# A graph and mixture-of-experts layer: first expert blocks placed inside the last GNN chunk, with two weight buffers in place of three

## Chip, cores and metric

The kernel runs on one core of a Trainium2 chip. The metric is the device time of one launch in microseconds (us), the median of several runs. Engines are named as the profile names them: PE (TensorE matmul), PEld (its weight load), DVE (VectorE), ACT (ScalarE), POOL (GpSimd) and SP (SyncE, which here issues most DMA transfers).

## What is computed

There are N = 3125 nodes with C = 256 features and 103125 sorted edges. The layer normalizes x, adds up each node's neighbours, runs a gated recurrent cell and a fully connected layer on the sum, adds a small attention-like mix, and then sends every node through two of eight experts. Cut to what matters:

```python
xn = _layernorm(x)
agg = segment_sum(xn[src], dst)
h = relu(agg @ W_rel + b_rel + xn @ W_root)
i, f, g, o = split(h @ W_ih.T + b_ih + b_hh, 4)
c = sigmoid(i) * tanh(g)
x = x + (sigmoid(o) * tanh(c)) @ W_fc + b_fc + mix(xn)
xt = _layernorm(x)
probs = softmax(xt @ Wr + br)              # 8 experts
top_p, top_idx = top_k(probs, 2)
weights = top_p / top_p.sum()
xe = _layernorm(xt) * ln_g[e] + ln_b[e]    # per expert e
y = gelu(xe @ W1[e] + b1[e]) @ W2[e] + b2[e]   # 256 -> 1024 -> 256
out = x + sum over the two chosen experts of weights * y
```

All of it is float32.

## The kernel before

**Stages.** The edge stage builds adjacency tiles and multiplies them with the nodes (L612 to L654), up to about 355 us. Then follows a conditional, `tc.If(total > 0)` at L656, a slow path for unsuitable edge lists that these inputs don't take. Then comes the GNN stage, in chunks of TQ = 4 tiles of P = 126 tokens (`chunk`, L720): six chunks of four tiles, and a seventh of one tile. Then a plan of blocks is made (L890 to L963), and then comes the expert stage (`block`, L970).

**One chunk.** PE computes hT from aggT (L737, with `root` added by DVE at L739), the gates (L747, with sigmoid and tanh on ACT at L749), and the output rows (L765, L768, added by DVE at L770). The rows are normalized (L204) and stored into `acc_dram` (L773), on which the experts later accumulate. The second half of a chunk, the routing, is a generator's remainder: it runs inside the next chunk's gates. It computes the logits (L795 on DVE; in the last two chunks L808 on PE, by way of the transposed lT), softmax and top two, counts with two small matmuls which slot of its expert each token gets (L856, L857; `first` is where an expert's slots begin, `seen` what has been handed out), and scatters each tile's rows into `xs_dram` by two indirect DMAs on POOL (L872, called puts here). Tokens of an expert e lie in rows e*R onward, in the order of arrival.

**One block.** A block is 256 rows of one expert. SP loads the weights w1 (L992), w2 (L993) and the bias b2s (L995), of 1024, 1024 and 128 KB, and the rows xs (L1006). PE transposes xs (L1010), DVE scales the result into xe (L1014), PE multiplies by w1 into PSUM (L1020), ACT applies Gelu into hf (L1022), PE multiplies by w2 (L1033), DVE adds b2s and multiplies by the gate (L1036, L1037), and POOL adds the result into `acc_dram` by an indirect DMA (L1038). Blocks 0 to 7 are the first 256 slots of the experts. The blocks from 8 on are given out by the plan, so their expert and place are read from a register, and after every fourth of them comes a half block of 128 rows. 24 full and four half blocks run in any case; the conditionals at L1050 and L1053 after them are not taken. The last step copies `acc_dram` to the output.

**Buffers.** The pool `ew` holds w1, w2 and b2s three times; `ffn` holds xs three times and its other tiles twice. PSUM has two `ps_tr`, three `ps_mm` and three `ps_o` buffers. The pools `gnn` and `rt` of the GNN stage end before `plan` and `ffn` begin, and their memory is used again.

**What sets the order.** The program is written in the order of the source; a scheduler then places each engine's instructions in one static order, by its own estimate of what is ready. Each engine and each queue works through its order one by one, so an instruction that waits holds up all that stand behind it on the same engine. SP's order around the change is: xT and root of chunk 0, xT of chunk 1, wrows, the conditional, base of two chunks, then the weights of blocks 0, 1 and 2 with root of chunk 1 between.

Of the kernel before, what the change touches and what calls it, by code (L numbers as in the profile page):

```python
# [9 lines left out]
F32 = mybir.dt.float32  # L10
# [8 lines left out]
C = 256  # L19
P = 126  # L20
T = 25
# [24 lines left out]
ROW = C + NE + 1  # L46
XROWS = NE * R + SB
KS = 2 * KC + KF

# [14 lines left out]
def gps_layer(  # L64
# [409 lines left out]
    first = keep.tile([128, 1, NE], F32, name="first")  # L474
    nc.gpsimd.tensor_scalar(first[:, 0, :], cols[:, :NE], float(R), None, op0=OP.mult)
    token = keep.tile([P, T], I32, name="token")
    nc.gpsimd.iota(token, pattern=[[P, T]], base=0, channel_multiplier=1)
# [235 lines left out]

    ew = ctx.enter_context(tc.tile_pool(name="ew", bufs=3, side="right"))
    with tc.tile_pool(name="gnn", bufs=1) as hp, tc.tile_pool(name="rt", bufs=2) as rp:
# [4 lines left out]
        def chunk(t0, pending):  # L720
# [21 lines left out]
            for m in range(KH):  # L742
# [12 lines left out]
                if m == 1 and n > 2 * P:  # L755

                    with tc.issue_after(mm.ins):
                        for _ in pending:
                            pass
            xl = rp.tile([P, TQ, C], F32, name="xl")  # L760
            rows = rp.tile([P, TQ, ROW], F32, name="rows")
            for i, t in enumerate(ts):
# [4 lines left out]
                for k in range(KC):  # L767
# [6 lines left out]
                              base[:, :nt, :])  # L774
            for _ in pending:
                pass
            yield
# [21 lines left out]
            else:  # L799
                lT = rp.tile([128, KC, CT], F32, name="lT", bufs=1)  # L800
                for k in range(KC):
# [46 lines left out]
            if ts[-1] == T - 1:  # L848
                nc.vector.tensor_scalar(chosen[:, nt - 1, :], chosen[:, nt - 1, :], valid, None,
                                        op0=OP.mult)  # L850
            prior = rp.tile([P, TQ, NE], BF16, name="prior")
            for i in range(nt):
# [10 lines left out]
            for r in range(2):  # L863
# [30 lines left out]
    with tc.tile_pool(name="plan", bufs=1) as lp:  # L894
# [68 lines left out]
        nc.vector.tensor_copy(used_i[:, 1:2], hends[:, 0, NE - 1:])  # L963


    SP = (mybir.EngineType.SP,)
    NH = SB // 128
    with tc.tile_pool(name="ffn", bufs=2) as fp:
        def block(b, half=False):

            nh = 1 if half else NH
            ns = 128 * nh
            if b < NE and not half:
                begin, e = b * R, b
                xs_b, w1_b, w2_b = xs_dram[begin:begin + SB, :], W1[e], W2[e]
                b2_b = b2[e:e + 1, :]
                is_e = None
            else:
                if half:
                    of, is_e = (hbegin_i, hwho_i), is_hwho[:, b:b + 1, :]  # L980
                    j = b
                else:
                    j = b - NE
                    of, is_e = (begin_i, who_i), is_who[:, j:j + 1, :]
                begin, e = (nc.values_load(v[0:1, j:j + 1], engines=SP, min_val=0, max_val=most)
                            for v, most in zip(of, (NE * R, NE - 1)))
                xs_b = xs_dram[ds(begin, ns), :]
                w1_b, w2_b = (w[ds(e, 1), :, :].rearrange("o r m -> (o r) m") for w in (W1, W2))
                b2_b = b2[ds(e, 1), :]
            w1 = ew.tile([128, KC, HID], F32, name="w1")  # L990
            w2 = ew.tile([128, KF, C], F32, name="w2")
            nc.sync.dma_start(w1, w1_b.rearrange("(k p) m -> p k m", p=128))  # L992
            nc.sync.dma_start(w2, w2_b.rearrange("(k p) m -> p k m", p=128))  # L993
            b2s = ew.tile([128, C], F32, name="b2s")
            nc.sync.dma_start(b2s, b2_b.to_broadcast([128, C]))  # L995
            if is_e is None:
                sm = small[:, :, b]
            else:
                all_ = fp.tile([128, KS, NE], F32, name="all_")
                nc.vector.tensor_tensor(all_, small,  # L1000
                                        is_e.to_broadcast([128, KS, NE]), OP.mult)
                sm = fp.tile([128, KS], F32, name="sm")
                nc.vector.tensor_reduce(sm, all_, AX.X, OP.add)
            lng, lnb, b1s = sm[:, :KC], sm[:, KC:2 * KC], sm[:, 2 * KC:]
            xs = fp.tile([128, NH, ROW], F32, name="xs", bufs=3)[:, :nh, :]
            nc.sync.dma_start(xs, xs_b.rearrange("(h p) c -> p h c", p=128))  # L1006
            pt = ps_tr()
            for k in range(KC):
                for h in range(nh):
                    nc.tensor.transpose(pt[:, k * ns + h * 128:k * ns + h * 128 + 128],  # L1010
                                        xs[:, h, 128 * k:128 * k + 128], ident)
            xe = fp.tile([128, KC, SB], F32, name="xe")[:, :, :ns]
            for k in range(KC):
                nc.vector.tensor_scalar(xe[:, k, :], pt[:, k * ns:(k + 1) * ns],  # L1014
                                        lng[:, k:k + 1], lnb[:, k:k + 1], op0=OP.mult, op1=OP.add)
            hf = fp.tile([128, KF, SB], F32, name="hf")[:, :, :ns]
            for m in range(KF):
                pm = ps_mm()[:, :ns]
                for k in range(KC):
                    nc.tensor.matmul(pm, w1[:, k, 128 * m:128 * m + 128], xe[:, k, :],  # L1020
                                     start=(k == 0), stop=(k == KC - 1))
                nc.scalar.activation(hf[:, m, :], pm, AF.Gelu, bias=b1s[:, m:m + 1])  # L1022
            for h in range(nh):
                if is_e is None:
                    gate = xs[:, h, C + e:C + e + 1]
                else:
                    gate = fp.tile([128, 1], F32, name="gate", bufs=4)
                    scr = fp.tile([128, NE], F32, name="scr", bufs=4)
                    nc.vector.scalar_tensor_tensor(scr, xs[:, h, C:C + NE], 1.0, is_e[:, 0, :],  # L1029
                                                   op0=OP.mult, op1=OP.mult, accum_out=gate)  # L1030
                po = ps_o()[:, :C]
                for m in range(KF):
                    nc.tensor.matmul(po, hf[:, m, 128 * h:128 * h + 128], w2[:, m, :],  # L1033
                                     start=(m == 0), stop=(m == KF - 1))
                y = fp.tile([128, C], F32, name="y", bufs=4)
                nc.vector.tensor_tensor(y, po, b2s, OP.add)  # L1036
                nc.vector.tensor_scalar(y, y, gate, None, op0=OP.mult)  # L1037
                nc.gpsimd.indirect_dma_start(  # L1038
                    out=acc_dram[:, :],
                    out_offset=bass.IndirectOffsetOnAxis(ap=xs[:, h, C + NE:].bitcast(I32), axis=0),  # L1040
                    in_=y, in_offset=None, compute_op=OP.add)

        for b in range(SURE):
            block(b)
            if b >= NE and (b - NE) % HSURE == HSURE - 1:
                block((b - NE) // HSURE, half=True)
        used = nc.values_load(used_i[0:1, 0:1], min_val=0, max_val=ND)  # L1047
        hused = nc.values_load(used_i[0:1, 1:2], min_val=0, max_val=NE)
        for b0, b1 in ((SURE, SURE + 2), (SURE + 2, NBLK)):
            with tc.If(used > b0 - NE):  # L1050
                for b in range(b0, b1):
                    block(b)
        with tc.If(hused > HSURE):  # L1053
            for b in range(HSURE, NE):
                block(b, half=True)
    nc.sync.dma_start(out, acc_dram[:N, :])
# [59 lines left out]
```

## Time and profile before

| | |
|---|---|
| median of 3 runs | 1149.16 us (1146.96 to 1151.12) |
| profiled execution | 1149.45 us, its span 1147.7 us |
| PE busy | 1057.1 us, 92% of the span |
| DVE, ACT, POOL busy | 553.6, 427.5, 169.7 us |
| L747 (gates), PE | 257.8 us, 672 passes |
| L1020 and L1033 (experts), PE | 189.4 and 184.2 us |
| DMA moved | 161.43 MB, 141 GB/s in the mean |
| weight loads w | 56 of 1024 KB |

A matmul in float32 appears as two passes, so 16 matmuls of a block's up-projection are "x32". In a row of the timeline the columns are start, duration over the merged instructions, engine, line, operation, output and inputs, shape, count, and in brackets the idle time of the engine before it with what ended that. Rows of one engine overlap a little, since a matmul's end is modelled and the next one starts before it. A row of stages has the stretch, its length, then busy time and count for PE, PEld, DVE, ACT and POOL, then the granted clock, the share of DMA time and GB/s. The granted clock is a share of TensorE's full speed. The page's chain of waits reaches back only from the end to 1120 us, so the stages have to be read one by one.

### The profile page before, as it was taken

The page shows a single profiled execution, that of the slowest core. Times are in us where ns is not written, and L with a number is a line of the kernel's source. Part 1 is how long each engine was busy: PE and PEld are TensorE (multiplying, and loading weights), DVE is VectorE, ACT ScalarE, POOL GpSimd, SP SyncE. Part 2 cuts the span into 40 slices and gives each one's busy share as a digit, 9 for nine tenths or more (in the row PEclk, how much of TensorE's full clock was granted, in tenths as well). Part 3 has the DMA queues.
Part 4 walks back from the last instruction along what each step waited for, and adds up shares of the span by engine and source line. Part 5 has one row for each costly group of instructions (what it writes and reads, how often), then busy time and mean ns, then how long its engine had stood idle before and what let it go on. Part 6 is the DMA issues. An engine that isn't in the chain of part 4 may idle for free. (4 is left out here: it accounts for less than half of the span.)

```text
span 1147.7 us, 15551 instructions
## 1 busy us (share of the span) xinstructions
PE 1057.1 (92%) x5613; PEld 807.3 (70%) x5613; DVE 553.6 (48%) x1767; ACT 427.5 (37%) x936; POOL 169.7 (15%) x153
## 2 busy tenths in 40 slices
PE   5799999999999999999999998299999999899992
PEld 2357988988996454545454557288888888788881
DVE  5757788788761184848383937411112222222210
ACT  3454755755732233334333336122222232222220
POOL 2220000000001002020202021212212222122221
PEclk9889999999999999999999999599999999999996
DMA  7884965963007521213121111157666676666734
GB/s 230 293 278 131 252 168 130 253 170 96 1 1 239 176 91 38 91 38 91 38 91 37 36 38 46 52 147 201 188 193 189 187 235 184 201 188 193 227 65 126
DMA packets 121148, 161.43 MB, mean 141 GB/s; under 512 B 9570, under 2 KB 109320, under 8 KB 120870
## 3 DMA queue, kind: packets, MB, share of 16 engines
q1 hardware_dynamic: 108156, 144.40, 41.0%
q0 software_dynamic: 12064, 15.08, 7.1%
q8 instruction: 49, 0.80, 0.3%
q10 hardware_dynamic: 840, 0.83, 0.2%
q14 instruction: 39, 0.32, 0.1%
HBM read 101.37 MB, written 62.10 MB: 142 GB/s over the span
## 5 line engine op out<-in xcount | busy, mean ns | idle before, releaser
L747 PE MATMUL ps_mm<-hT,wih 128*128 128x504 f32 (+1 forms) x672 | 257.8, 543 | 1.6 <-ACT act L749 1.6
L747 PEld LDWEIGHTS ps_mm<-hT,wih 128*128 128x128 f32 x672 | 120.3, 190 | 133.8 <-issue 127.9
L1020 PE MATMUL ps_mm<-xe,w 128*128 128x256 f32 (+1 forms) x896 | 189.4, 369 | 3.3 <-DVE xe L1014 3.3
L1033 PE MATMUL ps_o<-w,hf 128*128 128x256 f32 x832 | 184.2, 379 | 0.0
L1020 PEld LDWEIGHTS ps_mm<-xe,w 128*128 128x128 f32 x896 | 161.6, 192 | 27.0 <-DVE xe L1014 6.6
L630 PE MATMUL ps_o<-A,hi 126*128 126x252 f32 (+1 forms) x650 | 176.3, 305 | 0.8 <-ACT A L392 0.7
L1033 PEld LDWEIGHTS ps_o<-w,hf 128*128 128x128 f32 x832 | 157.8, 190 | 21.3
L630 PE MATMUL ps_o<-A,lo 126*128 126x252 f32 (+1 forms) x650 | 161.2, 281 | 0.0
L1022 ACT ACTIVATE hf<-ps_mm,sm 128x256 f32<-128x256 f32 (+1 forms) x160 | 71.7, 453 | 199.2 <-PE ps_mm L1020 197.5
L392 ACT CAST A<-ps_mm 126x450 fp32r<-126x450 f32 x175 | 93.8, 538 | 99.8 <-PE ps_mm L390 98.2
L1038 POOL DMA_INDIRECT acc_dram<-y,xs x52 | 80.4, 1546 | 318.8 <-DVE scr L1029 131.6
L630 PEld LDWEIGHTS ps_o<-A,hi 126*128 126x128 f32 x650 | 124.9, 192 | 2.8 <-ACT aggT L638 1.7
L384 DVE TENSOR_TENSOR hr<-two,rowT 128x756 bf16<-128x756 bf16 x175 | 95.9, 548 | 62.9 <-PE ps_mm L390 62.4
L630 PEld LDWEIGHTS ps_o<-A,lo 126*128 126x128 f32 x650 | 125.2, 193 | 0.0
L390 PE MATMUL ps_mm<-hk,hr 128*126 128x150 bf16 x1050 | 102.2, 233 | 12.7 <-DVE hk L384 12.4
L384 DVE TENSOR_TENSOR hk<-two,keyT 128x900 bf16<-128x900 bf16 x175 | 108.8, 622 | 0.0
L390 PEld LDWEIGHTS <-hr 128*126 128x126 bf16 x1050 | 91.2, 137 | 18.7 <-DVE hk L384 16.5
L1036 DVE TENSOR_TENSOR y<-ps_o,b2s 128x256 f32<-128x256 f32 x52 | 22.1, 425 | 163.9 <-PE ps_o L1033 163.9
L749 ACT ACTIVATE act<-ps_mm,bg 128x504 f32<-128x504 f32 (+1 forms) x84 | 52.6, 634 | 107.3 <-PE ps_mm L747 107.2
L795 DVE SCALAR_TENSOR_TENSOR scr<-xl,wrows 126x256 f32<-126x256 f32 x160 | 75.5, 472 | 3.3
L872 POOL DMA_INDIRECT xs_dram<-rows,at_i x50 | 52.6, 1052 | 127.9 <-DVE at_i L869 110.9
L1022 ACT ACTIVATE hf<-ps_mm,small 128x256 f32<-128x256 f32 x64 | 29.8, 474 | 76.4 <-PE ps_mm L1020 76.4
(250 smaller groups left out, 920.1 us busy)
## 6 DMA issues: line engine op xcount, KB each, us to landing
w<-in_W_dram SPq DMA_DIRECT2D x56, 1024.0 KB
xs_dram<-blank SPq DMA_DIRECT2D x3, 7022.5 KB
xs_dram<-blank SPq DMA_DIRECT2D x1, 6757.5 KB
xs<-xs_dram SPq DMA_DIRECT2D x24, 265.0 KB
root_dram<-hr SPq DMA_DIRECT2D x24, 252.0 KB
root<-root_dram SPq DMA_DIRECT2D x6, 1008.0 KB
b2s<-in_b_dram SPq DMA_DIRECT2D x28, 128.0 KB
xn_dram<-xn SPq DMA_DIRECT2D x5, 630.0 KB
```

The source lines that it names most:

```text
L384: row = nc.vector.tensor_tensor(to[:, :m], two[:, :, :w, :].to_broadcast([128, m, w, GH]), of[:, g:g + m, None, :].to_broadcast([128, m, w ...
L390: mm = nc.tensor.matmul(pa[:P, i * DT:(i + 1) * DT], hr[:, i, :, h], hk[:, i, :, h], start=(h == 0), stop=(h == GH - 1))
L392: copy = nc.scalar.copy(A[:, :, c0:c0 + m * D], pa[:P, :m * DT].rearrange("p (d t) -> p t d", t=T))
L630: last = nc.tensor.matmul(pg[k][:, :n], of[:, t, 128 * k:128 * k + 128], A[:, t, :n], start=(t == 0 and of is hi), stop=(t == T - 1 and of ...
L747: mm = nc.tensor.matmul(pm[:, :n], wih[:, k, i, 128 * m:128 * m + 128], hT[:, k, :n], start=(k == 0), stop=(k == KH - 1))
L749: nc.scalar.activation(act[:, i, :n], pm[:, :n], AF.Tanh if gate == 2 else AF.Sigmoid, bias=bg[:, gate, m:m + 1])
L795: nc.vector.scalar_tensor_tensor(scr, xl[:, i, :], 1.0, wrows[:, e, :], op0=OP.mult, op1=OP.mult, accum_out=lg[:, i, e:e + 1])
L872: put = nc.gpsimd.indirect_dma_start(out=xs_dram[:, :], out_offset=bass.IndirectOffsetOnAxis(ap=at_i[:w, i:i + 1], axis=0), in_=rows[:w, i ...
L1020: nc.tensor.matmul(pm, w1[:, k, 128 * m:128 * m + 128], xe[:, k, :], start=(k == 0), stop=(k == KC - 1))
L1022: nc.scalar.activation(hf[:, m, :], pm, AF.Gelu, bias=b1s[:, m:m + 1])
L1033: nc.tensor.matmul(po, hf[:, m, 128 * h:128 * h + 128], w2[:, m, :], start=(m == 0), stop=(m == KF - 1))
L1038: nc.gpsimd.indirect_dma_start(out=acc_dram[:, :], out_offset=bass.IndirectOffsetOnAxis(ap=xs[:, h, C + NE:].bitcast(I32), axis=0), in_=y, ...
```

## The change

The change has four parts. In the chunk after which 2520 tokens have been routed (the fifth), a new function `ahead` counts how many of the first 256 slots of experts 0 to 2 are still free, and moves `first` of these experts past them, so that no later token gets such a slot; it loads the 256 rows of each of these three experts on POOL's queue, after all puts so far. The block is now a generator, `parts_of`, that pauses after the transposes, in the middle and at the end of the up-projection, and after each half of the down-projection. In the last chunk two parts of block 0 are written ahead of the output rows, two behind them, three more (the end of block 0, the start of block 1) behind the top two, and the rest of blocks 1 and 2 after the puts. The weight pool is opened with two buffers instead of three, ahead of the GNN pools, and a pool `early` with one xe, one hf and two y for the early blocks stands beside it. lT shares the buffer of wrows. The pending routing of a chunk is finished before the output rows of the next.

```diff
+EARLY = 3
...
+    soon = keep.tile([128, NE], F32, name="soon")
+    nc.gpsimd.tensor_scalar(soon, cols[:, :NE], float(EARLY), None, op0=OP.is_lt)
+    empty = keep.tile([128, 1, NE], F32, name="empty")
...
-    ew = ctx.enter_context(tc.tile_pool(name="ew", bufs=3, side="right"))
+    def parts_of(b, fp, half=False, xs=None):
+        early = fp is fe
...
+        if xs is None:
+            xs = fp.tile([128, NH, ROW], F32, name="xs", bufs=3)[:, :nh, :]
+            nc.sync.dma_start(xs, xs_b.rearrange("(h p) c -> p h c", p=128))
...
+        yield
+        hf = fp.tile([128, KF, SB], F32, name="hf")[:, :, :ns]
+        for m in range(KF):
...
+            nc.scalar.activation(hf[:, m, :], pm, AF.Gelu, bias=b1s[:, m:m + 1])
+            if m in (KF // 2, KF - 1):
+                yield
+        for h in range(nh):
...
+            y = fp.tile([128, C], F32, name="y", bufs=2 if early else 4)
...
+            yield
+
+    def block(b, fp, half=False):
+        for _ in parts_of(b, fp, half):
+            pass
+
+    ew = ctx.enter_context(tc.tile_pool(name="ew", bufs=2, side="right"))
+    fe = ctx.enter_context(tc.tile_pool(name="early", bufs=1, side="right"))
...
+            for _ in pending:
+                pass
+            yield
             xl = rp.tile([P, TQ, C], F32, name="xl")
...
-            for _ in pending:
-                pass
             yield
...
-                lT = rp.tile([128, KC, CT], F32, name="lT", bufs=1)
+                lT = rp.tile([128, KC, CT], F32, name="lT", tag="wrows", bufs=1)
...
+            yield
             prior = rp.tile([P, TQ, NE], BF16, name="prior")
...
+                    puts.append(put)
+            if t0 + 3 * TQ > T >= t0 + 2 * TQ:
+                ahead()
+
+        def ahead():
+            pc = ps_tr()[:, :NE]
+            nc.tensor.matmul(pc, onesb, seen, start=True, stop=True)
+            nc.vector.tensor_scalar(empty[:, 0, :], pc, -1.0, float(SB), op0=OP.mult, op1=OP.add)
+            nc.vector.scalar_tensor_tensor(empty[:, 0, :], empty[:, 0, :], 0.0, soon,
+                                           op0=OP.max, op1=OP.mult)
+            nc.vector.tensor_tensor(first, first, empty, OP.add)
+            for e in range(EARLY):
+                xs = fe.tile([128, NH, ROW], F32, name=f"xs{e}")
+                load = nc.gpsimd.dma_start(
+                    xs, xs_dram[e * R:e * R + SB, :].rearrange("(h p) c -> p h c", p=128))
+                for put in puts:
+                    tc.add_manual_dep(load.ins, put.ins.name, mybir.DependencyInfo(
+                        mybir.DependencyClass.Sync, mybir.DependencyReason.DATA), reason="its rows")
+                blocks.append(parts_of(e, fe, xs=xs))
+
+        puts, blocks = [], []
         pending = iter(())
         for t0 in range(0, T, TQ):
             routed = chunk(t0, pending)
             next(routed)
-            pending = routed
-        for _ in pending:
+            if t0 + TQ < T:
+                next(routed)
+                pending = routed
+
+        parts = (part for of in blocks for part in of)
+        for n in (2, 2, 3):
+            for _ in range(n):
+                next(parts)
+            next(routed, None)
+        for _ in parts:
             pass
...
-        nc.vector.tensor_copy(held, pc)
+        nc.vector.tensor_tensor(held, pc, empty[:, 0, :], OP.add)
...
-        for b in range(SURE):
-            block(b)
+        for b in range(EARLY, SURE):
+            block(b, fp)
```

The steps of a block are otherwise those of before, moved ahead of the GNN stage in the source.

More of the change, by code (lines that the diff above doesn't have):

```diff
@@ L711, in gps_layer @@
                     nc.vector.tensor_tensor(col, pt[:, :len(ts) * P], col, OP.add)
-    ew = ctx.enter_context(tc.tile_pool(name="ew", bufs=3, side="right"))
+    SP = (mybir.EngineType.SP,)
+    NH = SB // 128
+    def parts_of(b, fp, half=False, xs=None):
+        early = fp is fe
+        nh = 1 if half else NH
+        ns = 128 * nh
+        if b < NE and not half:
+            begin, e = b * R, b
+            xs_b, w1_b, w2_b = xs_dram[begin:begin + SB, :], W1[e], W2[e]
+            b2_b = b2[e:e + 1, :]
+            is_e = None
+        else:
+            if half:
+                of, is_e = (hbegin_i, hwho_i), is_hwho[:, b:b + 1, :]
+                j = b
+            else:
+                j = b - NE
+                of, is_e = (begin_i, who_i), is_who[:, j:j + 1, :]
+            begin, e = (nc.values_load(v[0:1, j:j + 1], engines=SP, min_val=0, max_val=most)
+                        for v, most in zip(of, (NE * R, NE - 1)))
+            xs_b = xs_dram[ds(begin, ns), :]
+            w1_b, w2_b = (w[ds(e, 1), :, :].rearrange("o r m -> (o r) m") for w in (W1, W2))
+            b2_b = b2[ds(e, 1), :]
+        w1 = ew.tile([128, KC, HID], F32, name="w1")
+        w2 = ew.tile([128, KF, C], F32, name="w2")
+        nc.sync.dma_start(w1, w1_b.rearrange("(k p) m -> p k m", p=128))
+        nc.sync.dma_start(w2, w2_b.rearrange("(k p) m -> p k m", p=128))
+        b2s = ew.tile([128, C], F32, name="b2s")
+        nc.sync.dma_start(b2s, b2_b.to_broadcast([128, C]))
+        if is_e is None:
+            sm = small[:, :, b]
+        else:
+            all_ = fp.tile([128, KS, NE], F32, name="all_")
+            nc.vector.tensor_tensor(all_, small,
+                                    is_e.to_broadcast([128, KS, NE]), OP.mult)
+            sm = fp.tile([128, KS], F32, name="sm")
+            nc.vector.tensor_reduce(sm, all_, AX.X, OP.add)
+        lng, lnb, b1s = sm[:, :KC], sm[:, KC:2 * KC], sm[:, 2 * KC:]
+        if xs is None:
+            xs = fp.tile([128, NH, ROW], F32, name="xs", bufs=3)[:, :nh, :]
+            nc.sync.dma_start(xs, xs_b.rearrange("(h p) c -> p h c", p=128))
+        pt = ps_tr()
+        for k in range(KC):
+            for h in range(nh):
+                nc.tensor.transpose(pt[:, k * ns + h * 128:k * ns + h * 128 + 128],
+                                    xs[:, h, 128 * k:128 * k + 128], ident)
+        xe = fp.tile([128, KC, SB], F32, name="xe")[:, :, :ns]
+        for k in range(KC):
+            nc.vector.tensor_scalar(xe[:, k, :], pt[:, k * ns:(k + 1) * ns],
+                                    lng[:, k:k + 1], lnb[:, k:k + 1], op0=OP.mult, op1=OP.add)
+        yield
+        hf = fp.tile([128, KF, SB], F32, name="hf")[:, :, :ns]
+        for m in range(KF):
+            pm = ps_mm()[:, :ns]
+            for k in range(KC):
+                nc.tensor.matmul(pm, w1[:, k, 128 * m:128 * m + 128], xe[:, k, :],
+                                 start=(k == 0), stop=(k == KC - 1))
+            nc.scalar.activation(hf[:, m, :], pm, AF.Gelu, bias=b1s[:, m:m + 1])
+            if m in (KF // 2, KF - 1):
+                yield
+        for h in range(nh):
+            if is_e is None:
+                gate = xs[:, h, C + e:C + e + 1]
+            else:
+                gate = fp.tile([128, 1], F32, name="gate", bufs=4)
+                scr = fp.tile([128, NE], F32, name="scr", bufs=4)
+                nc.vector.scalar_tensor_tensor(scr, xs[:, h, C:C + NE], 1.0, is_e[:, 0, :],
+                                               op0=OP.mult, op1=OP.mult, accum_out=gate)
+            po = ps_o()[:, :C]
+            for m in range(KF):
+                nc.tensor.matmul(po, hf[:, m, 128 * h:128 * h + 128], w2[:, m, :],
+                                 start=(m == 0), stop=(m == KF - 1))
+            y = fp.tile([128, C], F32, name="y", bufs=2 if early else 4)
+            nc.vector.tensor_tensor(y, po, b2s, OP.add)
+            nc.vector.tensor_scalar(y, y, gate, None, op0=OP.mult)
+            nc.gpsimd.indirect_dma_start(
+                out=acc_dram[:, :],
+                out_offset=bass.IndirectOffsetOnAxis(ap=xs[:, h, C + NE:].bitcast(I32), axis=0),
+                in_=y, in_offset=None, compute_op=OP.add)
+            yield
@@ L963, in gps_layer @@
         nc.vector.tensor_copy(used_i[:, 1:2], hends[:, 0, NE - 1:])
-    SP = (mybir.EngineType.SP,)
-    NH = SB // 128
     with tc.tile_pool(name="ffn", bufs=2) as fp:
[L969 to L1041, printed above, removed]
-        for b in range(SURE):
-            block(b)
@@ L1045, in gps_layer @@
+        for b in range(EARLY, SURE):
+            block(b, fp)
             if b >= NE and (b - NE) % HSURE == HSURE - 1:
-                block((b - NE) // HSURE, half=True)
+                block((b - NE) // HSURE, fp, half=True)
         used = nc.values_load(used_i[0:1, 0:1], min_val=0, max_val=ND)
@@ L1051, in gps_layer @@
                 for b in range(b0, b1):
-                    block(b)
+                    block(b, fp)
         with tc.If(hused > HSURE):
             for b in range(HSURE, NE):
-                block(b, half=True)
+                block(b, fp, half=True)
     nc.sync.dma_start(out, acc_dram[:N, :])
```

## Prediction

> **What bounds the kernel now.** First the page's slices: TensorE at 9 nearly everywhere, so only its gaps matter, and the granted clock has one hole, 5 in slice 25. I then cut the span into stages (us, busy per engine, clock, DMA share, GB/s):
>
> ```profile
> 693.00:740.00 47.00, 21.61 (x165) 19.60 (x164) 29.33 (x162) 18.53 (x37) 12.47 (x10) 0.75 0.19 54
> 740.00:1126.00 386.00, 378.96 (x1832) 331.91 (x1832) 78.05 (x266) 102.79 (x225) 78.83 (x51) 0.99 0.64 179
> ```
>
> From 693 to 740, the last GNN chunk and the routing, TensorE works 21.6 of 47 us. TensorE's timeline shows what it waits for:
>
> ```profile
> 713.88 0.60 PE L768 MATMUL ps_o<-kvbd,xT 128*126 128x128 f32 x4
> 716.84 0.65 PE L211 MATMUL ps_tr<-ident,xl 126*128 126x126 f32 x2 [2.36 <-DVE xl L204]
> 722.60 0.19 PE L903 MATMUL ps_tr<-seen,onesb 126*128 126x8 bf16 x1
> 739.96 1.94 PE L1010 MATMUL ps_tr<-ident,xs 128*128 128x128 f32 x8 [17.17 <-DMA xs<-xs_dram]
> 741.70 4.00 PE L1020 MATMUL ps_mm<-xe,w 128*128 128x256 f32 x12
> ```
>
> The 17.17 us are scatter, landing, and load of xs. The last line is 12 matmuls in 4.00 us where later rows have 32 in 7.07: the clock is 0.50 until 744.2. Next the steady expert stage, where blocks go in pairs:
>
> ```profile
> 799.73 1.04 PE L1010 MATMUL ps_tr<-ident,xs 128*128 128x128 f32 x8
> 800.97 7.17 PE L1020 MATMUL ps_mm<-xe,w 128*128 128x256 f32 x32 [0.20 <-DVE xe L1014]
> 807.98 7.07 PE L1033 MATMUL ps_o<-w,hf 128*128 128x256 f32 x32
> 814.89 7.07 PE L1020 MATMUL ps_mm<-xe,w 128*128 128x256 f32 x32
> 828.70 1.04 PE L1010 MATMUL ps_tr<-ident,xs 128*128 128x128 f32 x8
> ```
>
> A pair takes 28.97 us: four times 6.91, and 1.34 for the transposes, the DVE step xe and the wait for it, paid once for two blocks. Last the start of the GNN stage, since the change moves the weight loads (SP's issues in the same timeline):
>
> ```profile
> 347.56 0.63 SPq L592 DMA_DIRECT2D xT<-xT_dram  x1
> 355.12 0.33 SPq L718 DMA_DIRECT2D wrows<-wr_dram  x1
> 356.19 7.00 PE L737 MATMUL ps_mm<-aggT,wrel 128*128 128x504 f32 x16 [1.16 <-DVEq L656]
> 359.97 0.86 SPq L122 DMA_DIRECT2D base<-in_x_dram  x2
> 360.07 1.27 DVE L739 TENSOR_TENSOR hT<-ps_mm,root 128x504 f32<-128x504 f32 x2 [4.68 <-SPq L656]
> 360.88 0.46 SPq L992 DMA_DIRECT2D w<-in_W_dram  x1
> 363.03 9.46 PE L747 MATMUL ps_mm<-hT,wih 128*128 128x504 f32 x22
> ```
>
> DVE's first step waits 4.68 us for SP at L656, the conditional that isn't taken. In both programs SP leaves that conditional only when all eight of its DMA counters have reached every transfer issued before it; here the last is wrows, whose traffic ends at 359.2.
>
> **Part 1, weights ahead of the conditional: +10.3 us.** With a third of the weight memory gone, the changed program issues w1, w2 and b2s of blocks 0 and 1 right after the second xT load, ahead of wrows and of the conditional; before, all weights came behind it. So SP, and DVE behind it, wait for them as well. Traffic: xT, root, xT end at 353.4 (1-us stretches). Then 2x(1024+1024+128) KB = 4.46 MB at 375 GB/s (mean of the stretches in which weights alone flow, 355 to 402) is 11.9 us, and wrows 1.03 MB 2.7 us: 368.0. From the end of wrows to DVE took 0.9, so DVE starts at 368.9, not 360.07. TensorE has three PSUM buffers there: three of four L737 groups end at 361.3, the fourth waits for DVE's first hT (0.66) until 369.65. That is 8.4 us idle, and a clock of 0.50 afterwards: it lasted 4.2 us after the gap at 740 and about 3 us after one of 3.15 us at 989 to 992. Half of some 3.9 us is lost, 1.9. TensorE is full for the rest of the GNN stage, so nothing gives this back. Bounds: 8 (at 405 GB/s, as xT had) and 15 (at 280, as at 363 to 367); zero is excluded by the counters. The weights' former slot, 361 to 387, had TensorE full already, so its freeing brings nothing.
>
> **Part 2, blocks 0 to 2 inside the last chunk: -20.8 us.** I lay the changed instruction order on the rows of before. Until 708.0 it is the same. Then: routing matmuls 0.26, four transposes of block 0 0.52, one L765 0.43, 32 passes of L747 3.67: 712.9. Six up-projections of block 0 (two passes of 0.216 each, 0.43) wait for the act evictions, to 715.5; with L765 and L768 between, all 16 are issued at 721.55. ACT needs four table loads between evictions hf5 (720.5) and hf7: sqrt, Gelu, sqrt, Gelu. A load row is 1.28 and the next ACTIVATE follows at once: hf6 at 723.85, hf7 at 727.2. The down-projection reaches hf7 at 724.85: a stall of 2.45. Here two rules of the Trainium skill differ from the trace. "ScalarE: Activation LUTs", What ACT_TABLE_LOAD costs, adds a drain of 1.38 to each load; then the four would take 5.5 us more, and so would the sum. Row: load at 700.49, 1.28 long, ACTIVATE at 701.78; I take the row. "TensorE: Matmul & The Clock Gate", Part 1, lets the clock fall after an idle window of about 3.4 us; by that the stall costs no clock. The row of 716.84 shows 0.50 from 716.9 on, after 2.36 us; I take the row, 1.6 us. So block 0's down-projection ends at 733.3, and the wait for y and xe of block 1 costs 1.7 more. Block 1 with the last routing matmuls ends at 750.1, block 2 at 763.9, and block 3's up-projection begins at 765.15. In before it begins at 785.92.
>
> What must be under cover for that: the final puts. Block 0's two acc scatters stand before them on POOL and need y at 735.2; the puts' addresses come at 740.2. In before the first of these two puts started at 724.00 and xs was issued at 736.90: 12.9. So xs is issued at 753 and lands (3 us) near 757, 7 us before TensorE comes. DVE's all_ waits for the puts too, and y of block 1 behind it until 752; three po buffers bear that until 757. The weights of block 2 are issued at 721 (w1) and 731 (w2), needed at 750. On SP, w1 of block 3 now stands ahead of xs of blocks 3 to 5 and waits for block 1's up-projection (743), which is earlier than the puts; its w2 follows at 755, needed at 772. The three POOL loads of xs wait for puts whose traffic ended at 677.9, and are read at 708.3; POOL has nothing else until 710.06. The matmul and three DVE steps of ahead (0.2 each) lie in chunk 5, where DVE idles up to 6 us at a time. lT in wrows' memory: last read 658, first written 698. No slot is padded: experts 0 to 2 have 676, 605 and 606 tokens in the first five chunks. All this I cost at nothing. Bounds of part 2: -24.9 (no stall of hf7, no clock loss) and -15.3 (the page's drains).
>
> **Part 3, the order in the expert stage: +7.6 us, and +1.** With two weight buffers, SP's w2 of block n stands ahead of xs of block n and waits for the end of block n-2. So the program has blocks 3 to 6 in two pairs, but transposes of each of the 17 full blocks from 7 and of the four halves alone. A group alone costs nearly what a pair's does, since DVE's y and xe set it: 1.13 (row 770.87) to 1.34, I take 1.28. Sum: 21 full x 13.82 = 290.2; two pairs 2.7; 17 x 1.28 = 21.8; four halves at 8.41 (915.61 to 924.01 has one with its own group) 33.6: 348.3 from block 3's transposes, 347.05 from its up-projection (1.24 later). In before it is 1125.39-785.92 = 339.5, and that includes 4.9 us at 989 to 997 where a pair's second xs was late, which goes. Bounds +4 (1.13 each) and +9.
>
> After a half block, xs of the next block has little time. It stands behind w2, which waits for the block ahead of the half: w2 starts 0.3 us after that block; then some 2 us to first data, 1.45 MB at 375 GB/s 3.9 us, the scatter between 1.3 us: 7.5 to 8 against the 8.4 of the half. I put 1 us for three places; bounds zero and 11 (rival below).
>
> **Sum.** TensorE ends at 765.15+347.05+10.3+1 = 1123.5, before 1125.4. The tail to the span's end, 22.3, stays: 1145.8. Outside the span lie 1.75 (1149.45-1147.7): 1147.6 against this execution's 1149.45. The median of the runs is 0.3 lower: 1147.3, 0.2% faster, within the 0.3% (3.4 us) that a measurement can tell from no change.
>
> **Rivals.** (a) Faster: the gain stands and its costs don't. For: part 1 rests on one wait at one place; if DVE's hT needed only root (landed 353.5), 10.3 go: 1137. Against: its wait names SP L656, not root. Likewise 1141 with hf7 and the lone groups at their low bounds. (b) Slower: xs after the half blocks. It decides at 8.4 us from the end of the block ahead; landing 2 us later costs 2 and a halved clock 1.6, three times, 10.8 instead of 1: 1157. For: the scatters and w2 share the queue engines then, and the stall of 3.15 at 992.72 had the same xs. Against: that one was issued only after its need. (c) That the early blocks don't run early: if their xs loads landed after 725 instead of before 700, the gap stays and parts 1 and 3 are left, 1167. For it speaks only the longest landing of a put, 10 us, far less than the 30 of cover.
>
> **Chances.** The case of the sum, 1143.5 to 1151.5, 0.5, of which 0.12 lies under 1145.7; (a) 0.22; (b) with smaller stalls of its kind 0.23; (c) 0.05. So faster 0.34, within 0.3% 0.38, slower 0.28. A range that leaves out half of (a) and half of (b) with (c): 1139 to 1156.
>
> **What would show it.** In the profile after: part 1, DVE's first hT near 369 and a gap of 8 us in TensorE before it, clock 0.50 behind it; part 2, no idle of over 3 us from 705 to 775 (10 later than my times), ACT table loads between hf rows; part 3, L1010 in groups of 4 with 0.6 to 0.8 idle before L1020. It is wrong if DVE starts at 360, if TensorE waits for xs of block 3, or if L1010 after a half waits for DMA.

## The result and the profile after

The changed kernel takes 1153.64 us (median of 16 runs, 1150.10 to 1158.77) against 1148.58 us for the kernel before on the same chips (16 runs, 1145.49 to 1153.94). The ratio is 1.0044, 95% interval 1.0029 to 1.0059: slower by 0.44%, some 5 us, where 1.9 us faster was forecast. The time lies inside the forecast's range of 1139 to 1156, but on the other side of no change.

The profiled execution hides most of that. It took 1150.1 us, the lowest of the 16, and its span of 1148.2 is only 0.5 longer than that of before. So I cut the span at three places of TensorE's timeline that both kernels have, and added the same cut of a second profile of the changed kernel, taken later (run `again`, span 1156.1):

| stage of TensorE, us | before | after | after, second profile |
|---|---|---|---|
| span's start to first matmul with wrel | 356.19 | 354.49 | 355.25 |
| from there to the last chunk's first | 337.19 | 351.95 | 352.35 |
| from there to block 3's up-projection | 92.54 | 71.31 | 74.31 |
| from there to the end of TensorE's work | 339.47 | 348.13 | 350.65 |
| span's end after that | 22.3 | 22.3 | 23.5 |

The first row, the edge stage, isn't edited by the change, and it varies by itself: from 351.4 to 356.2 over the twelve profiles of this document. Without it the first profile is 2.2 us longer than before and the second 9.3.

**The GNN stage's start** (timeline of the changed kernel: start, duration, what it is, and in brackets the idle time ahead of it with what ended it). SP's queue:

```profile
345.87 0.63 SPq L597 DMA_DIRECT2D xT<-xT_dram  x1
346.54 0.67 SPq L746 DMA_DIRECT2D w<-in_W_dram  x1
347.25 0.63 SPq L747 DMA_DIRECT2D w<-in_W_dram  x1
347.93 3.82 SPq L749 DMA_DIRECT2D b2s<-in_b_dram  x1
...
353.29 5.52 SPq L749 DMA_DIRECT2D b2s<-in_b_dram  x1
358.92 1.18 SPq L812 DMA_DIRECT2D wrows<-wr_dram  x1
370.69 0.86 SPq L123 DMA_DIRECT2D base<-in_x_dram  x2
```

DVE's first step and TensorE:

```profile
370.83 1.86 DVE L833 TENSOR_TENSOR hT<-ps_mm,root 128x504 f32<-128x504 f32 x3 [17.15 <-SPq L661]
```

```profile
354.49 5.31 PE L831 MATMUL ps_mm<-aggT,wrel 128*128 128x504 f32 x12 [1.15 <-DVEq L661]
371.57 3.73 PE L831 MATMUL ps_mm<-aggT,wrel 128*128 128x504 f32 x4 [11.77 <-DVE hT L833]
```

As the prediction has it, the weights stand ahead of wrows (358.92) and of the conditional, and DVE waits 17.15 us for SP at L661. From the first matmul with wrel to the first gate, TensorE now takes 20.60 us instead of 6.84. The size differs. Forecast was a wait for hT of 8.4; the row of 371.57 has 11.77. The transfers behind it, in stretches of the changed kernel (from:to, length, busy time and number per engine, then granted clock, share of the DMA engines' time, GB/s):

```profile
357.00:359.00 2.00, 2.00 (x6) 0.95 (x5) 0.00 (x0) 0.00 (x0) 0.00 (x0) 1.00 0.59 193
359.00:364.00 5.00, 0.80 (x2) 0.00 (x0) 0.00 (x0) 0.00 (x0) 0.00 (x0) 0.96 1.04 383
365.00:367.00 2.00, 0.00 (x0) 0.00 (x0) 0.00 (x0) 0.00 (x0) 0.00 (x0) 0.50 0.95 238
367.00:370.00 3.00, 0.00 (x0) 0.00 (x0) 0.00 (x0) 0.00 (x0) 0.00 (x0) 0.50 0.49 137
```

From 357 to 359 the rate halves, while SP stands in the second b2s issue for 5.52 us and wrows goes out only after it (that the late wrows is the cause isn't shown; see run 2). From 365 on the last megabyte trickles at 238 and 137 GB/s. Against the 375 of my sum, the first stretch lacks 2 x (375-193) = 364 KB and the last two 2 x 137 + 3 x 238 = 988 KB: together 3.6 us of transfer at 375, which is what hT's wait has too much (3.4). The rest is clock: 0.50 from 363.57 to 377.22, so the fourth wrel group takes 3.73 us (the three before it took 5.31 together), and about 2 us of the gates run at half speed. TensorE works 5.65 us at half clock, where the forecast had 3.9. All told 14.8 us, not 10.3.

**The last chunk.** Forecast -20.8, measured -21.2 in this profile, but not by the path that I laid out: a wait of 2.33 us for xe of block 3 stands in it, which I had at 0.2, and the stall at hf is 1.84 instead of 2.45 and costs no clock:

```profile
738.86 0.70 PE L791 MATMUL ps_o<-w,hf 128*128 128x256 f32 x2 [1.84 <-ACT hf L778]
739.40 0.38 PE L212 MATMUL ps_tr<-ident,xl 126*128 126x126 f32 x2
...
774.39 1.04 PE L765 MATMUL ps_tr<-ident,xs 128*128 128x128 f32 x8
777.75 7.17 PE L776 MATMUL ps_mm<-xe,w 128*128 128x256 f32 x32 [2.33 <-DVE xe L769]
```

**The expert stage** has the lone groups as forecast, each with some 0.64 us of waiting for xe; no half block is followed by a wait for xs. There are 17 groups of four transposes and four of two, as counted beforehand. Groups by shape (line, operation, count, then busy time, mean ns, then idle time before it and what ended it), the changed kernel:

```profile
L776 PE MATMUL ps_mm<-xe,w 128*128 128x256 f32 x768 | 172.4, 382 | 14.5 <-DVE xe L769 14.0 <-ACT hf L778 0.5
L776 PE MATMUL ps_mm<-xe,w 128*128 128x128 f32 x128 | 16.4, 282 | 2.5 <-DVE xe L769 2.5
```

17.0 us of idle time at the up-projections, 3.3 in the kernel before. Forecast 348.05 for the stage (347.05 and 1), measured 348.13.

What had to be found: whether the weights really are the price of the start, why that price is larger, and where the typical run has 3.5 us more than the profiled one.

### The profile page after: what moved, and what is told of

Same layout as the page of the kernel before. It is cut to its first block, busy times and chain, and to the rows that moved or that the text cites. A ratio compares the mean times of both kernels' runs of the same rounds, so it can differ in the third digit from the quotient of the medians.

```text
span 1148.2 us, 15546 instructions
## 1 busy us (share of the span) xinstructions
PE 1057.5 (92%) x5614; PEld 804.8 (70%) x5614; DVE 551.6 (48%) x1770; ACT 431.3 (38%) x940; POOL 171.6 (15%) x157
## 5 line engine op out<-in xcount | busy, mean ns | idle before, releaser
L776 PEld LDWEIGHTS ps_mm<-xe,w 128*128 128x128 f32 x896 | 159.1, 190 | 42.2 <-DVE xe L769 22.2
L831 PE MATMUL ps_mm<-aggT,wrel 128*128 128x504 f32 (+1 forms) x112 | 45.7, 560 | 12.9 <-DVE hT L833 11.8
```

## Experiments

Ratios are to the kernel before, run beside each version on the same chip; times are medians.

**1. Both blocks' weights held until the first gate matmul**, so that SP issues them behind the conditional:

```diff
+        loads = [nc.sync.dma_start(w1, ...), nc.sync.dma_start(w2, ...), nc.sync.dma_start(b2s, ...)]
+        if early and b < 2:
+            for load in loads:
+                tc.add_manual_dep(load.ins, gates[0].ins.name, ...)
```

> The changed kernel, with the weight and bias loads of blocks 0 and 1 waiting for the first gate matmul of chunk 0, so that SP issues them behind the untaken conditional. My theory: the 4.46 MB ahead of the conditional cost 13.8 us until the first gate and about 1 more at half clock, so this run is 13 to 15 us faster than the changed kernel, about 1139 us, ratio to the kernel before 0.990 to 0.993, and in its profile DVE adds hT again within 5.5 us of the end of the edge stage. Rival 1: the start is late for another reason (the new order of instructions, the lower pool), and the loads only fill a wait that is there anyway: then the time stays at that of the changed kernel, ratio 1.004. Rival 2: the held weights come too late or take bandwidth from the first chunk's own loads: part of the gain comes back as stalls in the first two chunks, ratio 0.996 to 1.000.

Measured: 1139.22 us (5 runs), ratio 0.991 (0.9892 to 0.9928). From the first wrel matmul to the last chunk it takes 337.37 us, 14.6 less than the changed kernel and within 0.2 of before; the time falls by 14.2 against the changed kernel's 1153.45 beside it (run 4). In its timeline TensorE has no gap any more:

```profile
353.65 7.00 PE L837 MATMUL ps_mm<-aggT,wrel 128*128 128x504 f32 x16 [1.15 <-DVEq L661]
360.49 34.81 PE L847 MATMUL ps_mm<-hT,wih 128*128 128x504 f32 x82
```

So the loads ahead of the conditional are the whole price of the start, and held back they cost nothing: they then flow while TensorE is full with the gates. Rivals 1 and 2 fall.

**2. Only block 1's weights held**, the dose (`b < 2` becomes `b == 1`):

> As the run before it, but only block 1's loads wait; block 0's 2.23 MB still go ahead of the conditional. If the price is that of the bytes (4.46 MB for 13.8 us, 3.1 us a MB), half of it stays: about 7 us slower than with both held, ratio to the kernel before about 0.998, hT about 7 us later than with both held. Rival: much of the price is SP, stuck at the bias load behind a full queue so that the router rows go out only at 358.9, and the slow end of the queue (DMA share 1.0 at 66 to 335 GB/s after 364 us); with 9 fewer megabytes-queued descriptors ahead the router rows go out at once, and the price falls by more than half: 2 to 4 us slower than with both held, ratio 0.993 to 0.995.

Measured: 1147.43 us (15 runs), ratio 0.9983 (0.9972 to 0.9994), 8.2 us over the run with both held. TensorE's rows:

```profile
352.76 5.31 PE L837 MATMUL ps_mm<-aggT,wrel 128*128 128x504 f32 x12 [1.15 <-DVEq L661]
362.95 3.73 PE L837 MATMUL ps_mm<-aggT,wrel 128*128 128x504 f32 x4 [4.88 <-DVE hT L839]
```

The first gate is 6.9 us later than with both held, against 13.8 with nothing held: half the bytes, half the price. wrows went out at 351.69 here, at once, and the price is still half, so SP's stand at b2s is not most of it; that rival falls. (What I expected there of the share, 1.0 at 66 to 335 GB/s, was misread: in the changed kernel it is 1.11 at 335, but 0.16 at 66.) Of the bracketed waits, 4.88 belongs to the first 2.23 MB and 6.89 more to the second, which is 5.9 at 375 GB/s and 1.0 over; the half-clocked fourth group (2 us) is paid with the first. The dip in the rate is here too, 264 and 186 GB/s from 355 to 357, long after wrows was issued. So what makes the dip stays open.

**3. Two weight buffers alone**, the kernel before with one number changed:

```diff
-    ew = ctx.enter_context(tc.tile_pool(name="ew", bufs=3, side="right"))
+    ew = ctx.enter_context(tc.tile_pool(name="ew", bufs=2, side="right"))
```

> The kernel before with two weight buffers in place of three and nothing else of the change. My theory: it takes the price of the expert stage (17 groups of transposes alone, about +8) and, as its order of instructions also puts the weights of blocks 0 and 1 ahead of the conditional, that of the start (+14 to 15), and none of the gain of the last chunk: about 1171 us, ratio 1.018 to 1.022. Rival 1: the start price comes from something else of the change (the early pool, the scatter order): ratio about 1.007. Rival 2: three buffers held more weights ahead of the conditional only in name and the expert stage's price belongs to the moved blocks: ratio 1.000 to 1.003.

Measured: 1172.66 us (4 runs), ratio 1.0203 (1.0185 to 1.0221). The number alone brings the start's price (352.07 us from wrel to the last chunk) and, from there to the end of TensorE's work, 442.3 us against 432.0 before. Of these 10.3 us, 9.1 lie behind the first up-projection of block 0, in the expert stage. The change's losses at the start and in the expert stage come from this number, not from the early blocks.

**4. The changed kernel again**, for a second profile:

> The changed kernel once more, for a second profile and for its time beside the others. The profile on hand was the fastest of 16 runs of it (1150.1 against a median of 1153.6), and in it the three terms come to +0.5. My theory: the terms of the start, the last chunk and the expert stage are the same again within 1 us each (+14.8, -21.2, +8.7), and what the median has more (about 3.5 us) lies in the edge stage before 353 us, whose length varies from run to run in both kernels. Rival: the start's price itself varies with the queues (13 to 18 us) and 14.8 was its low end; then the first gate is later against the edge stage's end in this profile. Ratio 1.003 to 1.006.

Measured: 1153.45 us (6 runs), ratio 1.0031 (1.0016 to 1.0046). My theory fell: the edge stage is not it, the first cut is 0.8 us later only. Nor is it much of the rival's: the start's price is 15.2, only 0.4 more. But block 3 is late. TensorE:

```profile
775.48 1.04 PE L765 MATMUL ps_tr<-ident,xs 128*128 128x128 f32 x8
781.91 9.70 PE L776 MATMUL ps_mm<-xe,w 128*128 128x256 f32 x32 [5.40 <-DVE xe L769]
```

and DVE, which is what it waits for:

```profile
768.08 0.26 DVE L754 TENSOR_TENSOR all__7771<-small,is_who 128x96 f32<-128x96 f32 x1 [10.31 <-DMA xs_dram<-rows,at_i]
769.08 0.42 DVE L794 TENSOR_TENSOR y<-ps_o,b2s 128x256 f32<-128x256 f32 x1
774.87 0.42 DVE L794 TENSOR_TENSOR y<-ps_o,b2s 128x256 f32<-128x256 f32 x1 [4.26 <-DMA acc_dram<-y,xs]
780.98 0.42 DVE L794 TENSOR_TENSOR y<-ps_o,b2s 128x256 f32<-128x256 f32 x1 [5.30 <-DMA acc_dram<-y,xs]
781.32 0.54 DVE L769 TENSOR_SCALAR xe<-ps_tr,small 128x256 f32<-128x256 f32 x1
```

Read DVE from below. xe of block 3 (781.32) stands behind y of block 2's second half (780.98). That y has waited 5.30 us for the scatter of a y before it, and the one before (774.87) 4.26 us: the early blocks have two y tiles, and one is free only when its scatter has landed. The scatters themselves go one after another, on POOL at 770.16, 775.54 and 781.61. They all began late, because DVE stood 10.31 us at the masks (L754) for the rows' scatters, and y of block 1 stood behind the masks. In the first profile the same rows have waits of 9.06, 3.98 and 3.84, and TensorE waited 2.33. Here it is 5.40, and 9.70 for an up-projection that takes 7.17 at full clock. The 3.1 us between the two waits are 1.3 by which the masks run later behind the start of the last chunk, and 1.8 by which the scatters follow each other more slowly.

**5. Four y tiles in the early blocks**, on the changed kernel and nothing else:

```diff
-            y = fp.tile([128, C], F32, name="y", bufs=2 if early else 4)
+            y = fp.tile([128, C], F32, name="y", bufs=4)
```

> The changed kernel with four y tiles in place of two in the blocks that run early; nothing else. In the second profile of the changed kernel DVE stands at y of block 2 until the scatter of block 1 has landed (5.30 us), block 3's xe is behind it on DVE, and TensorE stands 5.4 us and then runs 2.5 us slower at half clock; in the first profile the same wait was 2.33 us. My theory: this is what the median of the changed kernel has over its fastest run; with four tiles y waits for no scatter, block 3's up-projection begins within 1.5 us of its transposes, and the time falls by 3 to 6 us against the changed kernel: ratio to the kernel before 0.998 to 1.001. Rival: DVE stands there for the rows' scatters and its masks (L754, landed at 765.7 to 768.1), which four tiles don't shorten, so block 3 is late all the same: ratio 1.003 to 1.005.

Measured: 1146.66 us (22 runs), ratio 0.9995 (0.9984 to 1.0006). The changed kernel had 1.0044 and 1.0031, so this is 4 to 6 us, by ratios that were taken on different chips. In its profile the masks still wait for the rows' scatters, but no y waits for a scatter, and block 3 starts at once (DVE, then TensorE):

```profile
763.79 0.26 DVE L754 TENSOR_TENSOR all__7771<-small,is_who 128x96 f32<-128x96 f32 x1 [9.53 <-DMA xs_dram<-rows,at_i]
768.62 0.42 DVE L794 TENSOR_TENSOR y<-ps_o,b2s 128x256 f32<-128x256 f32 x1 [2.30 <-PE ps_o L791]
772.08 0.42 DVE L794 TENSOR_TENSOR y<-ps_o,b2s 128x256 f32<-128x256 f32 x1 [2.64 <-PE ps_o L791]
```

```profile
771.88 1.04 PE L765 MATMUL ps_tr<-ident,xs 128*128 128x128 f32 x8
773.11 7.17 PE L776 MATMUL ps_mm<-xe,w 128*128 128x256 f32 x32 [0.20 <-DVE xe L769]
```

The last chunk to block 3 takes 67.1 us: a gain of 25.4 over before. The rival (the masks alone) falls: they delay DVE, but only the two tiles hand that on to TensorE. All four profiles with two y tiles (`after`, `again`, runs 1 and 2) have TensorE waiting 2.33 to 5.40 us for xe of block 3; all with four and three early blocks (runs 5 to 9) have 0.20. Not all of the gain is the tiles', though. Against the first profile the stretch is 4.2 us shorter: 2.1 is this wait, and 2.1 is the stall at hf, which this profile doesn't have and which four y tiles don't explain (runs 9 and 10 have it again). Against the second, the wait is 5.2 less and 2.5 of half clock behind it are gone. With this one number the change as a whole is no slower than before.

**6. Both together** (held weights and four y tiles):

> The held weights of both blocks and four y tiles together. If the two prices are of two different waits, they add: 4.1 us of waiting for xe and 1.7 at half clock (the rows of the profile with held weights) off 1139.2, so about 1133 to 1136, ratio 0.986 to 0.989. Rival: as in the run before it, the masks behind the rows' scatters hold DVE anyway, and the ratio stays at 0.991.

Measured: 1132.00 us (6 runs), ratio 0.9877 (0.9852 to 0.9903). The intervals of this ratio and of run 1's (0.9892 to 0.9928) just overlap, so the profile has to decide: from the last chunk to block 3 it takes 67.1 us, 73.0 with held weights alone, and the wait for xe of block 3 is 0.20, not 4.08. The start keeps its gain (337.1). So the two prices add, and they are two different waits.

**7. xs ahead of the weights**, on run 6:

```diff
+        if xs is None:
+            xs = fp.tile([128, NH, ROW], F32, name="xs", bufs=3)[:, :nh, :]
+            nc.sync.dma_start(xs, xs_b.rearrange("(h p) c -> p h c", p=128))
         loads = [nc.sync.dma_start(w1, ...
...
-        if xs is None:
-            xs = fp.tile([128, NH, ROW], F32, name="xs", bufs=3)[:, :nh, :]
-            nc.sync.dma_start(xs, xs_b.rearrange("(h p) c -> p h c", p=128))
```

> The kernel before it, and in each block of the expert stage the load of xs is issued ahead of the weights, so that it does not stand behind a wait for a weight buffer; TensorE's order has then pairs of 8 transposes again and fewer groups alone (about 5 for 17). My theory: the expert stage's price (8.7 us) is the groups of 4 transposes that stand alone, 0.64 us of waiting for xe and their half-empty pipeline each, so 6 to 8 us come back: about 1127, ratio 0.980 to 0.983. Rival: the price is that two buffers let TensorE get to a block before its weights have landed, and pairs change nothing: ratio as in the run before it, 0.986 to 0.989. A second rival: SP stands at xs for the rows' scatters with block 3's weights behind it, and block 3 is late: slower than the run before it.

Measured: 1126.42 us (5 runs), ratio 0.9822 (0.9807 to 0.9838), some 6 us for run 6's 0.9877. Pairs are back, and the waits for xe go from 14.4 us (11.9 and 2.5) to 3.9, so the lone groups were most of the price: the expert stage takes 344.3 us, 348.1 in run 6. But they bring a wait that wasn't there, for xs after two of the half blocks (TensorE; groups, then the two places):

```profile
L782 PE MATMUL ps_mm<-xe,w 128*128 128x256 f32 x768 | 174.3, 385 | 3.7 <-DVE xe L775 3.1 <-ACT hf L784 0.5
L771 PE MATMUL ps_tr<-ident,xs 128*128 128x128 f32 x104 | 14.9, 278 | 6.3 <-DMA xs<-xs_dram 6.3
```

```profile
897.77 0.91 PE L771 MATMUL ps_tr<-ident,xs 128*128 128x128 f32 x4 [2.39 <-DMA xs<-xs_dram]
1033.79 0.66 PE L771 MATMUL ps_tr<-ident,xs 128*128 128x128 f32 x4 [3.00 <-DMA xs<-xs_dram]
1034.81 8.72 PE L782 MATMUL ps_mm<-xe,w 128*128 128x256 f32 x32 [0.36 <-DVE xe L775]
```

**8. Other pieces**, on run 7: (3, 1, 3) for (2, 2, 3), by which all Gelu of block 0 come ahead of the layernorm's square roots:

> The kernel before it with pieces of 3, 1 and 3 in place of 2, 2 and 3: all 8 Gelu of block 0 stand ahead of the square roots of the layernorm on ACT, so 4 table loads of 1.28 us go. My theory: the 1.84 us for which the down-projection waited on hf behind those loads goes, and some of it is lost again because the layernorm and the routing come 1 to 3 us later: 1 to 2 us faster than the run before it, ratio 0.978 to 0.982. Rival: the loads lie beside other work, and the later routing delays the rows' scatters and so block 3: 0 to 3 us slower than the run before it.

Measured: 1127.66 us (5 runs), ratio 0.9827 (0.9810 to 0.9844): no difference from run 7, so my theory missed. The profile has three table loads of 1.28 us fewer (34 for 37), not four, and they move nothing; the stretch to block 3 is 67.0 and 67.1 us. But run 7's profile had no wait for hf that could go, so this says only that the loads alone cost nothing there; and TensorE waits 0.5 us longer for xe of block 1 with the new pieces.

**9. Four xs tiles in the expert stage**, on run 7 (`bufs=3` becomes `bufs=4`):

> The fastest version so far (held weights, four y tiles, xs ahead of the weights) with four xs tiles in the expert stage in place of three. In the profile of that version TensorE stands for xs 2.39 and 3.00 us after two of the four half blocks and 0.89 after block 4, and one up-projection then runs 1.5 us longer at half clock. My theory: the load of xs stands on SP behind a weight load that waits for one of the two buffers, and a fourth tile lets it go one block earlier: 4 to 7 us faster, about 1121, ratio 0.975 to 0.979. Rival: the load is late because of the weight buffers' queue order itself (a half block takes half as long as its 2.2 MB of weights take to be replaced), and a fourth tile changes little: ratio 0.980 to 0.983.

Measured: 1123.27 us (5 runs), ratio 0.9778 (0.9764 to 0.9792), the fastest version, 2.2% under the kernel before. The wait after block 4 and one of the other two shrink, one of 2.27 stays. From block 3 to the end it takes 340.1 us, what it took before with three weight buffers (339.5). The gain of about 5 us is in the range I gave, again by ratios taken on two chips. The rival's sum was off: 2.2 MB of weights take 5.9 us at 375 GB/s, less than the 8.4 of a half block.

**10. Two early experts instead of three**, on run 7:

```diff
-EARLY = 3
+EARLY = 2
```

> The fastest version so far with only experts 0 and 1 early (EARLY 2 in place of 3): block 2 then reads its rows, with those of the last chunk among them, in the expert stage. My theory of the last chunk's gain: the rows' scatters of the last chunk land about 5 us after block 1 ends (747.5 against about 742 in the profile of the version with three), and block 2 is what covers that and the load behind it; without it TensorE stands 8 to 12 us and runs 2 us slower after it: 9 to 14 us slower than with three, ratio 0.990 to 0.994. Rival: two blocks cover the wait already and the third only moves work: ratio 0.980 to 0.984.

Measured: 1136.54 us (6 runs), ratio 0.9897 (0.9876 to 0.9917), 8.6 us slower than run 7, just under the 9 to 14. The wait that block 2 had covered is back:

```profile
754.59 1.94 PE L771 MATMUL ps_tr<-ident,xs 128*128 128x128 f32 x8 [7.92 <-DMA xs<-xs_dram]
756.32 8.18 PE L782 MATMUL ps_mm<-xe,w 128*128 128x256 f32 x32
```

TensorE stands 7.92 us, and the transposes take 1.94 for 1.04 at half clock. So the third block is not moved for nothing: it covers the landing of the last rows and the load of xs behind it.

## Why the prediction was wrong, by its steps

- **Part 1, the mechanism: right** (runs 1 and 2). **Its size: the step that failed first.** "4.46 MB at 375 GB/s ... is 11.9 us, and wrows 1.03 MB 2.7 us" and "half of some 3.9 us is lost, 1.9" gave +10.3; measured +14.8 and +15.2 in the two profiles. Of the missing 4.5 us, 3.4 are transfer (a dip while the last weights go, 193 GB/s, and a slow last megabyte at 238 and 137; in between the rate was as assumed), 1.0 is clock (half until 377.22, 5.65 us of work and not 3.9). A mean rate of a steady flow was used for a flow with a dip and an end; why it dips stays open. The given bounds, 8 and 15, held the first of the two.
- **Part 2, blocks in the last chunk: right in direction, and wrong in a step costed at nothing.** "DVE's all_ waits for the puts too, and y of block 1 behind it until 752; three po buffers bear that until 757" has the masks right (765.66 in the first profile is 752.6 once the 13.1 by which its last chunk starts later is taken off), but it stops one buffer too early. Behind po come the two y tiles, each held until its scatter lands, and behind y on the same engine xe of block 3. That is 2.1 us over the forecast's 0.2 in the first profile, and 5.2 with 2.5 of clock in the other. In the first profile the stall at hf was 1.84 with no clock lost, where 2.45 and 1.6 were put: 2.2 too dear, and the wait 2.1 too cheap. The two cancel, so the agreement with -20.8 is luck and no proof of the working. Run 5's profile has neither the wait nor the stall, and its gain of 25.4 lies near the 24.9 that was given for no stall and no clock loss: the other terms held.
- **The two choices between row and rule in Part 2.** No drain follows a table load in the changed kernel either (ACT's timeline):

```profile
735.43 1.28 ACT L198 ACT_TABLE_LOAD   x1
736.73 0.29 ACT L198 ACTIVATE rs<-mv,eps 126x1 f32<-126x1 f32 x1
737.04 1.28 ACT L778 ACT_TABLE_LOAD   x1
738.33 0.47 ACT L778 ACTIVATE hf<-ps_mm,small 128x256 f32<-128x256 f32 x1
```

  Each ACTIVATE comes 1.3 us after the start of its load, so the drain that the Trainium skill adds ("ScalarE: Activation LUTs", What ACT_TABLE_LOAD costs) doesn't show here, and the row was the right choice. With the clock neither choice holds: after the stall of 1.84 us in this profile full speed stayed and the loss of 1.6 didn't come, but after the same stall in runs 9 and 10 (1.92 and 1.84 us) the clock was 0.50 for 3.41 us. So the idle window of about 3.4 us of the skill's "TensorE: Matmul & The Clock Gate", Part 1, taken as the length of a gap, is too high for what these runs show; the list at the end has what they show instead.
- **Part 3: right in sum** (348.13 for 348.05; 350.65 in the second profile, 2.5 of it the half clock at block 3). The 1 us for xs after half blocks wasn't needed in this order; the same wait appeared once the pairs were back (run 7).
- **Rivals.** (a) fell: hT does wait for the conditional. (b), xs after the half blocks, wasn't what made it slower. (c) fell: the early blocks do run early. The case that came true, a wait on DVE behind scatters, was none of them.
- **The sum.** Stages of the first profile: 14.76-21.23+8.66 = +2.2, and -1.7 from an earlier first cut gives +0.5 in the span. Stages of the second: 15.16-18.23+11.18+1.2 (end) = +9.3, and -0.9: +8.4 in the span. Without the first cut their mean is 5.8, near the 5.1 by which the medians differ; two profiles are few for more.

Left open: why the stall at hf (1.7 to 1.9 us) is in the profiles of `after`, `again` and runs 1, 2, 9 and 10 and not in those of runs 5, 6 and 7, whose order on TensorE and ACT around it is the same. In the first, ACT's sixth Gelu begins only when all three groups of a row of 12 matmuls are done; in the second, when the first of them is (ACT in `after`, where the row begins at 731.67, then in run 5, where it begins at 731.26):

```profile
734.94 0.47 ACT L778 ACTIVATE hf<-ps_mm,small 128x256 f32<-128x256 f32 x1 [3.90 <-PE ps_mm L776]
```

```profile
732.33 0.47 ACT L778 ACTIVATE hf<-ps_mm,small 128x256 f32<-128x256 f32 x1 [1.70 <-PE ps_mm L776]
```

Runs 5 to 8 ran on one chip, runs 1, 2, 4, 9 and 10 on two others, so the chip and the change can't be told apart here.

## What to carry to other kernels

Taking a buffer away changes more than the reuse distance (how soon a buffer is needed again): here it let a scheduler move the first loads ahead of a conditional, whose wait counts every transfer issued so far, and that cost more (14.8 us) than the pairing it broke (8.7). When work is moved under cover, follow each in-order engine to the end of the chain (masks, y, y tile, scatter, xe) and ask of every tile on it how many there are and what frees it. And set one profile against the spread of the runs: the first one here was the fastest of sixteen, and in it a wait that varies was at its shortest.

## What the runs showed of the hardware

- In these traces the granted clock changes only at steps of 3.41 us, and half clock lasts whole steps: eight in `before` (716.76 to 744.07), four in `after` (363.57 to 377.22), two in `again` (from 780.24), one in run 1 (from 764.89). So the length of a gap alone doesn't decide: half speed followed gaps of 2.36 us (before, 716.84), 2.27 (run 9, 901.67) and 1.84 (run 10, 723.28), and full speed stayed after 1.84 and 2.33 (after) and 2.28 (run 10, 977.39).
- What goes with it is how much of a step TensorE worked, by the profile's modelled busy time. Between 345 and 1095 us of the twelve profiles, all 18 full-speed steps in which it was busy for at most 0.44 of the time were followed by half clock. With 0.46 it went once each way (the two stalls of 1.84 us). With more, full speed stayed in all but four steps (0.66 in run 7; 0.90 in runs 1, 3 and 8), which this reading doesn't explain.
- SP can stand in the issue of a transfer: behind two loads of w the b2s issues of the changed kernel took 3.82 and 5.52 us, and wrows behind them went out that much later. In its expert stage, where loads are spread, the same issue took 0.35 to 0.53. That a full queue makes the difference is likely and not shown.
- The DMA engines can be 95% busy at 238 GB/s (365 to 367 in the changed kernel) and 104% at 383 just before (359 to 364). The share says that they are occupied, not what they move.
- Accumulating scatters in a row on POOL began 5.4 and 6.1 us apart in the second profile (770.16, 775.54, 781.61) and 5.1 and 4.6 in the first. With nothing changed in the kernel this spread makes 1.8 of the 3.1 us between the two waits for xe (2.33 and 5.40).
